# A two-layer graph transformer: 250 instead of 500 nodes in the dense share of the graph convolutions

## The chip, the cores and the metric

The kernel runs on one core of a Trainium2 chip. The metric is the device time of one execution in microseconds (us). Engines go by their short names: PE is TensorE (matmuls; PEld is its weight load), DVE is VectorE, ACT is ScalarE, POOL is GpSimd, SP is SyncE, which only issues DMAs. DRAM is the chip's memory; SBUF and PSUM are the core's own memories.

## The reference

The input is `x`, 2500 nodes by 256 features, and 40000 edges (`src`, `dst`), sorted by `dst`. All is float32. Two layers follow each other; each adds to `x` a graph operator and an attention-like mixer, both taken of the layer-normed `x`, and then a mixture of experts.

```python
edge_index = jnp.stack([src, dst])
xn = _layernorm(x, axis=-1)
x = x + _L0_gnn_ref(xn, ...) + _L0_mix_ref(xn[None], ...)[0]
x = x + _L0_ffn_ref(_layernorm(x, axis=-1)[None], ...)[0]      # 8 experts, each token to 2
xn = _layernorm(x, axis=-1)
x = x + _L1_gnn_ref(xn, ...) + _L1_mix_ref(xn[None], ...)[0]
x = x + _L1_ffn_ref(_layernorm(x, axis=-1)[None], ...)[0]      # 8 experts, each token to 1
```

The change lies in `_L1_gnn_ref`, two graph convolutions in a row, which the kernel computes beside `_L1_mix_ref`, a transformer of four layers (linear attention, then a feed-forward net 256 to 1024 to 256):

```python
deg = in-degree + 1 (a self loop);  dis = rsqrt(deg);  norm = dis[src] * dis[dst]
h = segment_sum((x @ W1)[src] * norm, dst) + b1          # self loops among the edges
h = where(h >= 0, h, alpha * h)
h = segment_sum((h @ W2)[src] * norm, dst) + b2
```

## The kernel before, in words

The 2500 nodes are held as 20 tiles of P = 125 nodes, in 5 groups of GT = 4 tiles (GC = 500 nodes). X is the running sum in SBUF.

**Layer 0.** The edges are turned into adjacency matrices by one-hot products, one group of 500 destinations at a time, and multiplied with the split features (`neighbours`, L458). While group 0 is in work, `between` (L1074) also writes its adjacency matrix, with the identity added on its diagonal blocks for the self loops, to DRAM as float32: `adj0`, 20 blocks of 125 sources by 500 destinations (L708, L1088 to L1094). The other groups' matrices are not kept.

**Ranks.** For the nodes outside group 0, `rank_nodes` (L326) sorts by in-degree: a histogram over 64 bins, matmuls for the prefix sums, and one indirect DMA per tile that writes each node's record to its rank in DRAM (`byrank`, L374). The ranks are cut into rows of 128. `MOST` (L34) gives the longest neighbour list that each row is prepared for; `rank_edges` (L381) fetches as many edges for each rank, one indirect DMA per row (L401), and leaves the neighbours' numbers in `nbr` and the nodes' own in `node`. If some node had more edges than its row allows, the count would not add up (L415 to L427) and a slow path would run. These steps are generators, which the loops of layer 0 and of its experts advance (L1095, L1227).

**The convolutions.** Everything after L1254 belongs to them and to the transformer. `conv_in` (L1287) writes x @ W1 times `dis` to the DRAM table `tabs[0]`. Each convolution then sums rows of its table in two ways:

- `dense` (L1272) for the 500 nodes of group 0: for each of the 20 source tiles it loads the adjacency block (`e`) and the table rows (`t`) and makes four products of 125 by 125 with 125 by 256 (L1281) into two PSUM tiles. It is cut into ten steps, and each transformer layer takes five of them (L1560, L1650).
- `gathers` (L1299) for the other 2000: for each row of 128 ranks, one indirect DMA for the node itself and one per neighbour place, 128 table rows of 1 KB each (L1313), on POOL's queue. They come in steps of SUM = 4; DVE adds each step to the first (L1325), then folds the four into one (L1329, L1331). POOL runs up to LEAD = 4 steps ahead, in LEAD + 1 buffers. `finish` then writes the row's sums: in the first convolution through `rectified` (L1340, bias and leaky rectifier) to `tabs[1]`, in the second to `sums2`, each with one indirect DMA (L1335).

The second convolution starts when the first one's last rows are written. After the fourth layer `conv_out` (L1387) takes the sums group by group: group 0 straight from PSUM (L1393), the others from `sums2` by a DMA on POOL's queue (L1395); it scales, transposes, multiplies by W2 and adds to X. The last mixture of experts follows.

**The order of the work** beside the transformer is dealt out by a clock that exists only while the program is traced. Each gather step has a due time: GATHER = 1.27 times the gathers so far (plus one per row), plus LANDING = 12, counted from the convolution's start; the second starts SEAM = 30 after the first's last step. The transformer calls `conv_step(now)` (L1369) at many places, and there all steps are emitted that are due:

```python
conv_step(LAYER * l - 0.6 * AHEAD * (NG - 1 - g) / NG)                                 # L1503, keys
conv_step(LAYER * l + AHEAD * i / NT * 0.7)                                            # L1552, context
conv_step(LAYER * l + AHEAD + (LAYER - 1.6 * AHEAD) * (g + step / (nj + GT)) / NG)     # L1604, feed-forward
```

So LAYER = 237 says how many units of that clock a transformer layer lasts. What a step puts on DVE stands in DVE's queue, in order, between the transformer's own instructions. Whatever is left at the end is emitted at L1671, ahead of `conv_out`.

Of the kernel before, what the change touches and what calls it, by code (L numbers as in the profile page):

```python
# [10 lines left out]
F32 = mybir.dt.float32  # L11
# [3 lines left out]
ALU = mybir.AluOpType  # L15
AX = mybir.AxisListType
# [3 lines left out]
D = 256  # L20
# [13 lines left out]
MOST = (42, 24, 22, 21, 19, 18, 18, 17, 16, 15, 15, 14, 13, 12, 11, 10)  # L34
# [7 lines left out]
LAYER = 237.0  # L42
# [24 lines left out]
def gps_kernel(ctx: ExitStack, tc: tile.TileContext, a, out):  # L67
# [258 lines left out]
    def rank_nodes(pool):  # L326

        nt = NT - GT
# [3 lines left out]
        V.tensor_scalar(upto, cnt[:, GT:NT], float(NBIN - 1), None, ALU.min)  # L332
# [6 lines left out]
        for g in range(NG - 1):  # L339
            ps = psum2.tile([128, 2, GT, NBIN], F32, tag="cx", name="ps")  # L340
            flat = oh[:, g * GT:(g + 1) * GT, :].rearrange("p i b -> p (i b)")
            T.matmul(ps[:P, 0].rearrange("p i b -> p (i b)"), below, flat, start=True, stop=True)
            T.matmul(ps[:, 1].rearrange("p i b -> p (i b)"), ones, flat, start=True, stop=True)
            for k in range(GT):
                V.tensor_tensor(rank[:, g * GT + k, :], ps[:P, 0, k, :], full[:P], ALU.add)
                V.tensor_tensor(full, ps[:, 1, k, :], full, ALU.add)
            yield
# [16 lines left out]
        G.tensor_copy(rec[:, :, 0:1], token[:, GT:, None])  # L364
        G.tensor_copy(rec[:, :, 1:2], cnt[:, NT + GT:2 * NT, None])
        G.tensor_copy(rec[:, :, 2:3], dis[:, GT:, None])
# [14 lines left out]
    def rank_edges(pool):  # L381
# [36 lines left out]
        V.tensor_reduce(hits[:P, 1:2], cnt[:, 0:GT], AX.X, ALU.add)  # L418
# [289 lines left out]
    adj0 = dram.tile([P, NT, GC], F32, name="adj0")  # L708
# [358 lines left out]
    for g in range(NG):  # L1067
# [6 lines left out]
        def between(k):  # L1074
# [179 lines left out]
    with tc.tile_pool(name="hid", bufs=8) as hid, tc.tile_pool(name="conv", bufs=1) as conv:  # L1254
# [17 lines left out]
        def dense(tab, sums):  # L1272

            for i in range(0, NT, 2):
                t = hid.tile([128, 2 * D], F32, tag="h", name="t")[:P].rearrange("p (k d) -> p k d", k=2)
                move(nc.sync, t, by_node(tab)[:, i:i + 2, :])
                for k in range(2):
                    e = hid.tile([128, 2 * D], F32, tag="h", name="e")[:P, :GC]
                    move(nc.sync, e, adj0[:, i + k, :])
                    for d in range(GT):  # L1280
                        T.matmul(sums[d // 2][:, d % 2, :], e[:, d * P:(d + 1) * P], t[:, k, :],  # L1281
                                 start=(i + k == 0 and d % 2 == 0), stop=(i + k == NT - 1 and d % 2 == 1))
# [71 lines left out]
        def first_group(sums):  # L1354

            by2 = conv.tile([P, GT], F32, name="by2")
            V.tensor_tensor(by2, dis[:, 0:GT], dis[:, 0:GT], ALU.mult)
            for d in range(GT):
# [706 lines left out]
```

## Time and profile before

| | us |
|---|---|
| median of three runs | 1825.29 (1821.66 to 1827.47) |
| the profiled execution | 1823.58 |
| its span (first to last instruction) | 1821.6 |
| mean granted PE clock | 0.978 |

Stretches of the profiled execution, from the span's start, with what PE and POOL were busy in each:

| stretch, us | what runs | PE | POOL |
|---|---|---|---|
| 0 to 300 | layer 0: scan, graph operator, mixer, gates, ranks | 261.7 | 108.6 |
| 300 to 490 | first mixture of experts | 169.5 | 88.1 |
| 490 to 594 | keys, context, attention of transformer layer 0 | 94.9 | 41.5 |
| 594 to 764 | feed-forward of layer 0 | 169.0 | 131.9 |
| 764 to 843, 843 to 1015 | layer 1: attention, feed-forward | 75.8, 169.7 | 60.7, 111.3 |
| 1015 to 1095, 1095 to 1265 | layer 2 | 76.2, 169.3 | 49.0, 127.4 |
| 1265 to 1350, 1350 to 1520 | layer 3 | 78.2, 169.6 | 65.8, 77.0 |
| 1520 to 1550 | `conv_out` | 24.6 | 0.2 |
| 1550 to 1822 | second mixture of experts | 260.0 | 81.3 |

PE is the busiest engine, 94% of the span. "Busy" counts an instruction's own time; the pauses between POOL's gathers, which issue the next DMA, count as idle. A releaser is what ended an engine's idle time, as inferred from the semaphores.

### The profile page before, as it was taken

The page shows a single profiled execution, that of the slowest core. Times are in us where ns is not written, and L with a number is a line of the kernel's source. Part 1 is how long each engine was busy: PE and PEld are TensorE (multiplying, and loading weights), DVE is VectorE, ACT ScalarE, POOL GpSimd, SP SyncE. Part 2 cuts the span into 40 slices and gives each one's busy share as a digit, 9 for nine tenths or more (in the row PEclk, how much of TensorE's full clock was granted, in tenths as well). Part 3 has the DMA queues.
Part 4 walks back from the last instruction along what each step waited for, and adds up shares of the span by engine and source line. Part 5 has one row for each costly group of instructions (what it writes and reads, how often), then busy time and mean ns, then how long its engine had stood idle before and what let it go on. Part 6 is the DMA issues. An engine that isn't in the chain of part 4 may idle for free. (4 is left out here: it accounts for less than half of the span.)

```text
span 1821.6 us, 24708 instructions
## 1 busy us (share of the span) xinstructions
PE 1718.5 (94%) x8081; PEld 1256.1 (69%) x8081; DVE 1005.7 (55%) x2906; ACT 655.3 (36%) x1170; POOL 942.7 (52%) x942
## 2 busy tenths in 40 slices
PE   4889999898799999999999999999999998999998
PEld 3646667787687667786776886676867767446767
DVE  8777744333554467576566374574646536333323
ACT  5743312222551434433335324343424331443220
POOL 2004483365217777777772666777777510144222
PEclk8999999999899999999999999999999999999999
DMA  5121156778436534554331664567543210621100
GB/s 141 57 60 44 37 169 197 241 222 233 131 107 170 97 93 112 165 146 143 98 102 49 195 120 138 158 176 202 156 139 92 73 50 33 216 65 48 32 21 29
DMA packets 131697, 216.59 MB, mean 119 GB/s; under 512 B 32876, under 2 KB 97570, under 8 KB 131303
## 3 DMA queue, kind: packets, MB, share of 16 engines
q0 software_dynamic: 51264, 111.78, 23.6%
q1 hardware_dynamic: 77990, 99.17, 18.4%
q10 hardware_dynamic: 2304, 3.94, 1.0%
q8 instruction: 70, 1.15, 0.3%
q14 instruction: 69, 0.56, 0.1%
HBM read 169.44 MB, written 47.79 MB: 119 GB/s over the span
## 5 line engine op out<-in xcount | busy, mean ns | idle before, releaser
L1313 POOL DMA_INDIRECT piece<-tab,nbr x574 | 591.8, 1031 | 204.4 <-issue 155.2
L1609 PE MATMUL mm<-xT,w 128*128 128x500 f32 x640 | 290.2, 596 | 2.8 <-ACT xT L487 2.8
L1620 PE MATMUL mm<-w,h 128*125 128x256 f32 x1280 | 288.0, 379 | 0.1
L1620 PEld LDWEIGHTS mm<-w,h 128*125 128x125 f32 x1280 | 238.0, 188 | 43.2 <-issue 8.8
L1609 PEld LDWEIGHTS mm<-xT,w 128*128 128x128 f32 x640 | 121.8, 195 | 119.4 <-issue 106.7
L1612 ACT ACTIVATE h<-mm,bf 128x500 f32<-128x500 f32 x160 | 106.8, 675 | 199.6 <-PE mm L1609 199.5
L1325 DVE TENSOR_TENSOR piece<-piece 128x1024 f32<-128x1024 f32 (+3 forms) x130 | 146.2, 1127 | 11.9 <-DMA piece<-tab,nbr 11.5
L465 PE MATMUL pa<-edges,xb 125*128 125x500 bf16 x600 | 138.7, 383 | 5.5 <-DVEq L959 3.6
L1622 DVE TENSOR_TENSOR tok<-tok,mm 125x256 f32<-125x256 f32 x80 | 33.5, 418 | 136.5 <-PE mm L1620 136.3
L1029 POOL DMA_INDIRECT back<-yo,xs x60 | 60.2, 1004 | 92.1 <-DVE yo L1027 52.7
L1577 DVE TENSOR_TENSOR tok<-tok,po 125x256 f32<-125x256 f32 x80 | 30.1, 418 | 138.2 <-PE po L1574 137.8
L465 PEld LDWEIGHTS <-xb 125*128 125x128 bf16 x600 | 58.6, 101 | 68.4 <-issue 11.5
L1012 PE MATMUL mm<-xc,wt 128*128 128x128 f32 x688 | 88.2, 283 | 15.5 <-DMA wt<-in_expert_in_dram 13.0
L1012 PEld LDWEIGHTS mm<-xc,wt 128*128 128x128 f32 x688 | 83.7, 198 | 17.4 <-issue 7.7
L1016 ACT ACTIVATE h<-mm,wt 128x128 f32<-128x128 f32 x172 | 49.1, 368 | 118.0 <-issue 65.4
L809 ACT CAST edges<-mm 125x500 bf16<-125x500 f32 x100 | 65.1, 790 | 70.6 <-PE mm L806 70.5
L494 ACT ACTIVATE tok<-tok,less,rstd 125x256 f32<-125x256 f32 x140 | 72.6, 591 | 38.4 <-DVE less L492 33.7
L1022 PE MATMUL py<-w,h 128*128 x344 | 82.8, 385 | 1.8 <-ACT h L1016 1.8
L487 ACT ACTIVATE xT<-mm,mixc 128x500 f32<-128x500 f32 x80 | 57.2, 765 | 68.1 <-PE mm L482 66.5
L1971 PE MATMUL py<-wd,taken 128*128 x368 | 80.9, 380 | 0.5 <-DVE taken L1961 0.5
L1499 PE MATMUL mm<-wa,xT 128*125 128x256 f32 x320 | 77.8, 398 | 1.9 <-ACT xT L487 1.2
L1971 PEld LDWEIGHTS py<-wd,taken 128*128 128x128 f32 x368 | 69.7, 190 | 11.3 <-issue 1.4
(484 smaller groups left out, 3010.9 us busy)
## 6 DMA issues: line engine op xcount, KB each, us to landing
wt<-in_expert_in_dram SPq DMA_DIRECT2D x43, 514.0 KB
sorted<-nothing SPq DMA_DIRECT2D x5, 2031.2 KB
piece<-tab,nbr POOLq DMA_INDIRECT x574, 3.1
e<-adj SPq DMA_DIRECT2D x40, 218.8 KB
w<-in_L_mix_W_dram SPq DMA_DIRECT2D x8, 1024.0 KB
wd<-in_L_ffn_Wd_dram SPq DMA_DIRECT2D x8, 1024.0 KB
t<-tab SPq DMA_DIRECT2D x20, 224.0 KB
adj<-wide SPq DMA_DIRECT2D x20, 218.8 KB
```

The costliest lines, as they stand in the source:

```text
L465: T.matmul(pa[c], table[:, k, n, c * 128:(c + 1) * 128], edges[:, k, :], start=(k == 0 and n == 0), stop=(k == NT - 1 and n == 2))
L494: S.activation(rows[:, k, :D], src[:, lo + k, :D], AF.Identity, bias=less[:, k:k + 1], scale=rstd[:, k:k + 1])
L809: S.copy(o.rearrange("p s (n d) -> p n s d", d=BD), ps[:P].rearrange("p (n s d) -> p n s d", n=BD, d=BD))
L1012: T.matmul(ps[:, j * TS:(j + 1) * TS], wt[:, c * F0 + j * 128:c * F0 + (j + 1) * 128], xc[:, c * TS:(c + 1) * TS], start=(c == 0), stop=(c ...
L1022: T.matmul(ps, h[:, j * TS:(j + 1) * TS], w2[:, ds(e, 1), j, :], start=(j == 0), stop=(j == NJ - 1))
L1313: G.indirect_dma_start(out=t[:, i, :], out_offset=None, in_=tab, in_offset=bass.IndirectOffsetOnAxis(ap=by, axis=0))
L1325: V.tensor_tensor(total[:, :m, :], total[:, :m, :], t[:, :m, :], ALU.add)
L1499: T.matmul(ps[:, k * D:(k + 1) * D], hT[:, c, (i + k) * P:(i + k + 1) * P], wk[:, c, :], start=(c == 0), stop=(c == 1))
L1609: T.matmul(ps, w1[:, c, j * 128:(j + 1) * 128], fT[:, c, g * GC:(g + 1) * GC], start=(c == 0), stop=(c == 1))
L1612: S.activation(h, ps, AF.Gelu, bias=bf[:, l, j:j + 1])
L1620: last["product"] = T.matmul(ps, hh[j][:, k * P:(k + 1) * P], w2[:, j, :], start=(j == 0), stop=(j == nj - 1)).ins
L1971: T.matmul(ps, h[:, j * TS:(j + 1) * TS], wd[:, ds(e, 1), j, :], start=(j == 0), stop=(j == nj - 1))
```

## The change

The dense share covers the first ND = 2 tiles (250 nodes) in place of the first group of four (500). The nodes from 250 on are ranked and gathered: 2250 in 18 rows of 128 in place of 2000 in 16 (2000 / 128 = 15.6, 2250 / 128 = 17.6), and `MOST` gets two more entries: it sums to 320 in place of 287. The adjacency in DRAM is half as wide, as are its copies and loads; `dense` makes two products per source tile in place of four; `first_group` rectifies two tiles in place of four. `rank_nodes` has a half-full fifth round, in one step of the generator with what follows. `conv_out` now also fetches the second half of group 0 from `sums2` by a DMA on POOL's queue. LAYER goes from 237 to 253, so the clock that deals out the steps runs faster against the transformer.

```diff
-MOST = (42, 24, 22, 21, 19, 18, 18, 17, 16, 15, 15, 14, 13, 12, 11, 10)
+MOST = (42, 24, 22, 21, 20, 19, 18, 17, 17, 16, 15, 15, 14, 14, 13, 12, 11, 10)
+ND = 2
+DC = ND * P
...
-LAYER = 237.0
+LAYER = 253.0
...
-        nt = NT - GT
+        nt = NT - ND
...
-        for g in range(NG - 1):
+        for lo in range(0, nt, GT):
+            n = min(GT, nt - lo)
...
-            yield
+            if n == GT:
+                yield
...
-    adj0 = dram.tile([P, NT, GC], F32, name="adj0")
+    adj0 = dram.tile([P, NT, DC], F32, name="adj0")
...
-                w = odd.tile([P, GC], F32, tag="wide", name="wide", bufs=3)
-                S.copy(w, edges[:, k, :])
-                if k < GT:
+                w = odd.tile([P, DC], F32, tag="wide", name="wide", bufs=3)
+                S.copy(w, edges[:, k, :DC])
+                if k < ND:
...
-                    e = hid.tile([128, 2 * D], F32, tag="h", name="e")[:P, :GC]
+                    e = hid.tile([128, 2 * D], F32, tag="h", name="e")[:P, :DC]
                     move(nc.sync, e, adj0[:, i + k, :])
-                    for d in range(GT):
+                    for d in range(ND):
                         T.matmul(sums[d // 2][:, d % 2, :], e[:, d * P:(d + 1) * P], t[:, k, :],
...
-            for d in range(GT):
+            for d in range(ND):
                 o = conv.tile([128, D], F32, tag="sums", name="sums", bufs=3)[:P]
...
+            lo = ND if g == 0 else 0
+            move(nc.gpsimd, s[:, lo:, :], by_node(sums2)[:, g * GT + lo:(g + 1) * GT, :])
+            V.tensor_tensor(s[:, lo:, :], s[:, lo:, :], by[:, lo:, :].to_broadcast([P, GT - lo, D]), ALU.mult)
             if g == 0:
-                for c in range(2):
-                    V.tensor_tensor(s[:, 2 * c:2 * c + 2, :], twice[0][c], by[:, 2 * c:2 * c + 2, :].to_broadcast([P, 2, D]), ALU.mult)
-            else:
-                move(nc.gpsimd, s, by_node(sums2)[:, g * GT:(g + 1) * GT, :])
-                V.tensor_tensor(s, s, by.to_broadcast([P, GT, D]), ALU.mult)
+                for c in range(0, ND, 2):
+                    n = min(2, ND - c)
+                    V.tensor_tensor(s[:, c:c + n, :], twice[0][c // 2][:, :n, :], by[:, c:c + n, :].to_broadcast([P, n, D]), ALU.mult)
```

More of the change, by code (lines that the diff above doesn't have):

```diff
@@ L331, in rank_nodes @@
         upto = pool.tile([P, nt], F32, name="upto")
-        V.tensor_scalar(upto, cnt[:, GT:NT], float(NBIN - 1), None, ALU.min)
+        V.tensor_scalar(upto, cnt[:, ND:NT], float(NBIN - 1), None, ALU.min)
         oh = pool.tile([P, nt, NBIN], F32, name="oh")
@@ L338, in rank_nodes @@
         yield
-        for g in range(NG - 1):
+        for lo in range(0, nt, GT):
+            n = min(GT, nt - lo)
             ps = psum2.tile([128, 2, GT, NBIN], F32, tag="cx", name="ps")
[L341 to L345, printed above, removed]
+            flat = oh[:, lo:lo + n, :].rearrange("p i b -> p (i b)")
+            T.matmul(ps[:P, 0, :n].rearrange("p i b -> p (i b)"), below, flat, start=True, stop=True)
+            T.matmul(ps[:, 1, :n].rearrange("p i b -> p (i b)"), ones, flat, start=True, stop=True)
+            for k in range(n):
+                V.tensor_tensor(rank[:, lo + k, :], ps[:P, 0, k, :], full[:P], ALU.add)
                 V.tensor_tensor(full, ps[:, 1, k, :], full, ALU.add)
-            yield
+            if n == GT:
+                yield
         upper = full[:P]
@@ L363, in rank_nodes @@
         G.memset(rec, 0.0)
-        G.tensor_copy(rec[:, :, 0:1], token[:, GT:, None])
-        G.tensor_copy(rec[:, :, 1:2], cnt[:, NT + GT:2 * NT, None])
-        G.tensor_copy(rec[:, :, 2:3], dis[:, GT:, None])
+        G.tensor_copy(rec[:, :, 0:1], token[:, ND:, None])
+        G.tensor_copy(rec[:, :, 1:2], cnt[:, NT + ND:2 * NT, None])
+        G.tensor_copy(rec[:, :, 2:3], dis[:, ND:, None])
         none = pool.tile([128, 4], F32, name="none")
@@ L417, in rank_edges @@
         V.tensor_reduce(hits[:, 0:1], hit, AX.X, ALU.add)
-        V.tensor_reduce(hits[:P, 1:2], cnt[:, 0:GT], AX.X, ALU.add)
+        V.tensor_reduce(hits[:P, 1:2], cnt[:, 0:ND], AX.X, ALU.add)
         V.tensor_tensor(hits[:, 0:1], hits[:, 0:1], hits[:, 1:2], ALU.add)
@@ L1277, in dense @@
                 for k in range(2):
-                    e = hid.tile([128, 2 * D], F32, tag="h", name="e")[:P, :GC]
+                    e = hid.tile([128, 2 * D], F32, tag="h", name="e")[:P, :DC]
                     move(nc.sync, e, adj0[:, i + k, :])
-                    for d in range(GT):
+                    for d in range(ND):
                         T.matmul(sums[d // 2][:, d % 2, :], e[:, d * P:(d + 1) * P], t[:, k, :],
-                                 start=(i + k == 0 and d % 2 == 0), stop=(i + k == NT - 1 and d % 2 == 1))
+                                 start=(i + k == 0 and d % 2 == 0), stop=(i + k == NT - 1 and (d % 2 == 1 or d == ND - 1)))
                 if i + 2 == NT and tab is tabs[0]:
@@ L1354, in first_group @@
         def first_group(sums):
-            by2 = conv.tile([P, GT], F32, name="by2")
-            V.tensor_tensor(by2, dis[:, 0:GT], dis[:, 0:GT], ALU.mult)
-            for d in range(GT):
+            by2 = conv.tile([P, ND], F32, name="by2")
+            V.tensor_tensor(by2, dis[:, 0:ND], dis[:, 0:ND], ALU.mult)
+            for d in range(ND):
                 o = conv.tile([128, D], F32, tag="sums", name="sums", bufs=3)[:P]
```

## The prediction

> **What bounds the kernel now.** I read the page's busy shares first, then the stretches of the four transformer layers, where the convolutions run, then POOL's groups inside each convolution, and last POOL's and DVE's waits. Page, busy shares and the two dense rows:
>
> ```profile
> PE 1718.5 (94%) x8081; PEld 1256.1 (69%) x8081; DVE 1005.7 (55%) x2906; ACT 655.3 (36%) x1170; POOL 942.7 (52%) x942
> ```
>
> The stretches; each line is attention or feed-forward of one layer (busy time of PE, PEld, DVE, ACT, POOL):
>
> ```profile
> 594.00:764.00 170.00, 168.97 (x660) 118.25 (x658) 102.61 (x297) 67.22 (x106) 131.89 (x126) 0.99 0.45 107
> 764.00:843.00 79.00, 75.81 (x375) 63.34 (x376) 59.27 (x134) 30.95 (x50) 60.70 (x61) 1.00 0.61 173
> 1015.00:1095.00 80.00, 76.18 (x379) 63.75 (x377) 50.00 (x110) 28.49 (x45) 49.00 (x49) 0.98 0.70 155
> 1265.00:1350.00 85.00, 78.22 (x379) 65.25 (x378) 54.43 (x118) 28.90 (x45) 65.79 (x64) 0.97 0.62 173
> ```
>
> PE is full in the feed-forward (169.0 of 170) and loses 3 to 7 us per attention stretch. So PE sets the length. But 52% is a poor picture of POOL. Its groups in the first convolution (540 to 967) and in the second (997 to 1449):
>
> ```profile
> L1313 POOL DMA_INDIRECT piece<-tab,nbr x287 | 297.1, 1035 | 87.5 <-issue 76.8 <-DMA piece<-tab,nbr 1.5 <-DVE neg L1347 0.9
> L1335 POOL DMA_INDIRECT tab<-sums,node x14 | 16.8, 1201 | 4.7 <-issue 3.4 <-DVE sums L1348 0.7 <-DVE fk L1424 0.3
> ...
> L1313 POOL DMA_INDIRECT piece<-tab,nbr x287 | 294.6, 1027 | 116.9 <-issue 78.3 <-DVE piece L1325 18.1 <-DVE qs L1545 10.3
> L1335 POOL DMA_INDIRECT sums<-sums,node x14 | 14.3, 1023 | 4.3 <-issue 3.0 <-DVE tok L1577 0.6 <-DVE tok L1622 0.3
> ```
>
> Almost all of its idle time is "issue", 0.30 us before every gather: back to back, a gather costs 0.95 + 0.30 us and more. In the first convolution POOL never waits longer than that: it is full from 540 to 966, as full as PE. The order of time at the turn between the convolutions shows where it has air:
>
> ```profile
> 964.99 0.95 POOL L1313 DMA_INDIRECT piece<-tab,nbr  x1 [0.30 <-issue]
> 966.64 1.01 POOL L1335 DMA_INDIRECT tab<-sums,node  x1 [0.71 <-DVE sums L1348]
> 973.84 1.01 POOL L1335 DMA_INDIRECT tab<-sums,node  x1 [6.18 <-DVE y L176]
> 993.69 0.98 POOL L1335 DMA_INDIRECT tab<-sums,node  x1 [18.84 <-DVE y L178]
> 998.25 0.99 POOL L1313 DMA_INDIRECT piece<-tab,node  x1 [3.57 <-DMA tab<-sums,node]
> ```
>
> 28 us lie there, since the last steps stand late in DVE's queue. At the end the last scatter goes out at 1476 and the feed-forward ends at 1520: 44 us of air. DVE's side:
>
> ```profile
> DVE piece L1325 <- DMA piece<-tab,nbr: 11.5, 5, 6.1
> ```
>
> DVE waits for a gather 11.5 us in all, in five places. So two engines run in step, and the change moves work from PE to POOL.
>
> **The change, part by part.**
>
> *Removed from PE.* L1281 has 76.0 us in 320 records (two per float32 product), 19.3 us in each attention stretch; half is 38.0 us, 9.5 per layer. Some of these products fill holes there, so the gain lies between 9.5 and 5 (the 3.2 to 6.8 us of holes a stretch grow by what filled them); I take 8, hence 32 us. If nothing else waited, the feed-forward of layer 3, ended at 1519.6, would end at 1487.6.
>
> *Added to POOL: the gathers.* 320 - 287 + 2 = 35 more per convolution, and two more scatters. First convolution before: 540.35 to 965.94 is 425.6 us; 13 scatters of 1.20 + 0.30 are 19.5, which leaves 406.1 / 303 = 1.340 per gather. After: 338 x 1.340 + 15 x 1.50 = 475.4, so its gathers end at 1015.8, 50 us later. Second before: 998.25 to 1447.44 is 449.2; 13 scatters of 1.32 are 17.2 and waits for buffers and landings 18.1 + 10.3 + 3.5 = 31.9, which leaves 1.320 per gather; after, 338 x 1.320 + 15 x 1.32 = 466.0. Bounds of the price: 1.256 (bare, no DVE instruction in the way) and 1.37 (eight more adds of L1325, 73 for 65, that each stop POOL for their whole 1.21 us: 9.7 / 338 = 0.03 more). I take 1.34 and 1.32, since the same DVE lines run beside them.
>
> The long gathers are those that start under a DVE add with both inputs in SBUF: 0.95 us bare, 1.96 us at 603.16 under L1325 (603.07 to 604.29). In the first convolution the excess is 297.1 + 16.6 - 303 x 0.953 = 25 us over 65 adds, 0.38 each; 8 more adds are 3 us, and the price per gather above has them. The Trainium skill, "SBUF — State Buffer", section Who interferes with whom, says that DVE with two SBUF inputs and a reading GpSimd exclude each other for the whole instruction; this speaks against the change. By that rule alone 8 adds of 1.21 us would cost up to 10 us a convolution in place of 3.
>
> *The turn.* Last add to first gather of the second convolution took 998.25 - 989.9 = 8.4 us; with a landing 2.1 us after the gather's end, the second starts at 1015.8 + 2.1 + 8.4 = 1026.3, against 998.25. The 28 us of air are gone.
>
> *The steps dealt out.* The last step of the second convolution is due at 958 of the clock's 988 units (before 864 of 924). In a feed-forward 189 units now pass in some 170 us, so a gather is due every 1.27 x 170 / 189 = 1.14 us and POOL delivers one in 1.34: over the 149 gathers due there POOL falls behind by 30 us, of which its lead of about 25 us (a piece landed at 966 was added at 990) takes the first part. Then DVE waits in its queue for the landing, and behind the waiting add stand attention's sums (L1577), the statistics (L187), and behind those ACT's rows (L494) and PE's transposes (L482), which wait now already: PE is held. The attention stretches (64 units in some 70 us) give little back. At the second's start its first adds are due late and POOL waits for buffers: before 6.4 and 7.1 us, now some 10. So its gathers end at 1026.3 + 466.0 + 10 = 1502.3.
>
> *The end, two ways.* Over the table: from last add (1473.4) to the rows for `conv_out` landed (1484.4) 11.0 us passed; after, 1502.3 + 2.1 + 11.0 = 1515.4. Over PE: the last point where a late DVE holds PE is the statistics of group 4, at 928 units; 30 units are 23 gathers, 31 us, so POOL's side is met at 1502.3 - 31 + 2.1 = 1473.4; one add (1.2) and the chain as before (L1577 at 1472.7 to L482 at 1481.0, 8.3) give 1482.9, and the rest of the layer (1481.0 to 1519.6, 38.6) gives 1521.5. The later one counts: +1.9 us against 1519.6.
>
> *DVE.* 16 more adds of 1.13 us and four more pairs of folds (0.69 and 0.42) in 980 us, of which it works 570: hidden, except that an add in the chain above delays it by 1.2. Landings come up to 7 us late (longest wait 6.1), and in step with POOL each counts once. Between 0 and 8 us; I take 3.
>
> *Ranks.* Two more record scatters (1.19 + 0.30 each) in POOL's fullest early stretch (71.5 of 100 us), two more edge gathers (1.0 + 0.3 each) between the experts' scatters, two small DVE pairs of 0.45 us, a half matmul round: between 0 (PE does other work there) and 6; I take 1.5. The two further generator steps fit into the loop's 23 calls (21 needed).
>
> *The rest.* Adjacency copies half as wide (ACT, 13.2 us of CASTs halved, beside a PE that waits 1.9 us for ACT there), half the block loads on SP's queue (5 MB less), two fewer `rectified`, one more table load for group 0 on POOL's queue (0.7 us twice), whose landing is in the 1515.4: -1 to +1, taken as 0. If that cover is gone, because the loads land after the feed-forward, `conv_out` waits for them.
>
> *Sum.* 1.9 + 3 + 1.5 = +6.4 on the profiled execution's 1823.6 (span 1821.6 and 2.0 around it): 1830. That execution lies 1.7 us under the median of the runs, 1825.3, so I forecast 1832.
>
> **The rivals.**
>
> *POOL keeps up, PE's gain comes through* (the other side). If gathers came at the bare 1.256, the first would end at 540.35 + 338 x 1.256 + 22.5 = 987.4, the second at 987.4 + 10.5 + 444.3 + 10 = 1452, and PE would set the end at 1488 to 1500: 1795 to 1805. It decides at a mean price of about 1.31, where POOL's two chains are 17 us shorter. For it: a waiting DVE does less beside the gathers. Against: the adds that lengthen gathers all stay.
>
> *Waits pass to PE whole.* If every late add holds PE until the last one, the 30 units behind the last step (27 us of feed-forward) follow the landing at 1504.4 plus add: 1533, +13, with the small terms +18: 1843; with a price of 1.35, 1852. For it: the transposes have no reserve (L482 waits for ACT's rows 19.9 us in all). Against: in group 4 PE and ACT run 14 us without DVE.
>
> *The late adds stay hidden.* DVE is idle 40% and catches up between chains; then the table alone counts, 1515.4: -4, with 1.5 for the ranks 1823.
>
> *It isn't what it says.* A row of ranks with more edges than MOST would run the slow path. The reference's edges, sorted by in-degree in 18 rows from node 250 on, start rows with 32, 22, 21, 20, 19, 18, 18, 17, 16, 16, 15, 15, 14, 13, 13, 12, 11, 9: none is over. No chance given.
>
> **How the numbers follow.** Forecast 0.50 (its own range 1824 to 1840), POOL keeps up 0.21, waits pass whole 0.18, late adds hidden 0.11. A measurement tells some 0.3%, 5.5 us, from no change: 1819.8 to 1830.8. Faster: 0.21 and a sliver, 0.22. Same: 0.11 and 0.15 of the forecast's 0.50, about 0.26. Slower: 0.52. The range leaves out the upper tail of the last case and the far half of the fast one: 1810 to 1852.
>
> **What would show it.** Right: 676 gathers at 1.31 to 1.35 us with no wait for L1325's buffers in the feed-forward; the second convolution's first gather at 1020 to 1032, its last at 1495 to 1510; DVE's waits for pieces up from 11.5 to over 60 us; PE under 165 of 170 us busy in the feed-forwards, L1281 at 38 us. Wrong: a gather price near 1.26; adds moved late in DVE's queue so that PE stays full and POOL ends alone after the feed-forward; first scatters of layer 0's experts visibly later.

## The result, and the profile after

The changed kernel takes 1877.57 us (median of 4 runs, 1875.72 to 1878.49) against 1824.76: slower by 2.74%, ratio 1.0274 with a 95% interval of 1.0255 to 1.0292. The forecast, 1832 in 1810 to 1852, had the sign and an eighth of the size. The profiled execution took 1878.3 us, its span 1876.3, at a mean granted clock of 0.955 (before 0.978).

The page's busy shares:

```profile
PE 1706.5 (91%) x7925; PEld 1238.4 (66%) x7925; DVE 1026.8 (55%) x2934; ACT 651.6 (35%) x1170; POOL 1034.5 (55%) x1022
```

PE is 12 us less busy, not 38, and 67 us more idle. Where, the stretches say (start and end; length; busy time and instructions of PE, PEld, DVE, ACT, POOL; granted clock; DMA share; GB/s): first the four feed-forwards, then the attention of layers 1 to 3.

```profile
595.00:787.00 192.00, 176.93 (x663) 122.09 (x663) 106.71 (x307) 68.67 (x109) 149.03 (x142) 0.94 0.44 106
871.00:1057.00 186.00, 173.13 (x658) 119.74 (x658) 109.84 (x319) 69.78 (x111) 133.55 (x129) 0.95 0.36 101
1135.00:1324.00 189.00, 175.88 (x662) 122.07 (x662) 102.53 (x293) 65.64 (x103) 137.64 (x132) 0.94 0.55 159
1402.00:1572.00 170.00, 169.84 (x656) 118.35 (x656) 87.84 (x199) 57.64 (x86) 122.68 (x117) 0.99 0.35 99
787.00:871.00 84.00, 69.59 (x331) 57.44 (x331) 56.45 (x126) 29.58 (x48) 65.10 (x63) 0.91 0.52 150
1057.00:1135.00 78.00, 67.31 (x337) 56.02 (x335) 45.57 (x105) 28.07 (x44) 45.14 (x48) 0.96 0.64 130
1324.00:1402.00 78.00, 67.34 (x333) 55.76 (x334) 51.68 (x114) 28.43 (x45) 59.55 (x61) 0.96 0.55 158
```

The loss has one address: the first three feed-forwards are 191.3, 185.7 and 188.4 us long, before 170.7, 172.6 and 170.4. That is 52 us of the 54.7 by which the two profiled spans differ. About 36 us of it are more idle time, the rest matmuls that run at a clock of 0.94 and not 0.99. The fourth feed-forward is full, as before. The second surprise stands in the last three lines. PE's work in the attention stretches fell by 6, 9 and 10 us, since half of the dense products are gone, and yet these stretches take 84.9, 78.2 and 78.1 us, before 78.8, 79.6 and 84.2: 1 us gained in all.

Why, the end of such a stretch shows. Layer 2, PE before (two lines), then PE and DVE after (start, duration, what; in brackets the idle time before it and what ended it):

```profile
1082.50 7.07 PE L1281 MATMUL da<-t,e 125*125 125x256 f32 x32
1092.08 2.16 PE L482 MATMUL mm<-ident,tok 125*128 125x125 f32 x8 [2.51 <-ACT tok L494]
...
1121.29 3.19 PE L1539 MATMUL mm<-wq,xT 128*125 128x256 f32 x14
1132.49 2.16 PE L486 MATMUL mm<-ident,tok 125*128 125x125 f32 x8 [8.02 <-ACT tok L498]
...
1119.76 0.75 DVE L1582 TENSOR_TENSOR tok<-tok,po 125x256 f32<-125x256 f32 x2 [1.93 <-PE po L1579]
1123.57 1.19 DVE L1329 TENSOR_TENSOR piece<-piece 128x1024 f32<-128x1024 f32 x1
1129.30 1.22 DVE L1329 TENSOR_TENSOR piece<-piece 128x1024 f32<-128x1024 f32 x1
1131.58 0.16 DVE L496 SCALAR_TENSOR_TENSOR less<-mv,rstd 125x4 f32<-125x4 f32 x1
```

From attention's sums (L1582) to `less` (L496) DVE works for 12.0 us without a pause, mostly at the statistics and softmaxes of the transformer itself, and waits for no gather. PE needs the rows that follow for its transposes (L486). Before, dense products filled that time; now PE stands there. In front of the feed-forwards of layers 1 to 3 these holes are 8.0, 8.0 and 8.2 us, before 1.5, 2.5 and 2.5.

The waits of the whole execution (engine, line, what it waited for: us in all, times, longest), before 33.7, 11.5, 19.9, 20.2 and 18.1 us in this order:

```profile
ACT tok L498 <- DVE less L496: 73.0, 25, 14.6
DVE piece L1329 <- DMA piece<-tab,nbr: 64.3, 13, 11.7
PEld mm L486 <- ACT tok L498: 49.0, 29, 8.6
ACT b L1348 <- DVE sums L1349: 44.5, 10, 16.0
POOL piece L1317 <- DVE piece L1329: 35.3, 8, 15.5
```

DVE waits for gathers, ACT's rows for DVE, PE for ACT's rows (the holes just shown are in these sums too); and POOL, which should be the engine that is late, waits 35 us for DVE. How a wait for a gather reaches PE is seen in order of time, in layer 1's feed-forward, POOL, DVE, ACT and PE:

```profile
1027.39 1.84 POOL L1317 DMA_INDIRECT piece<-tab,nbr  x1 [0.30 <-issue]
1038.29 1.00 POOL L1339 DMA_INDIRECT tab<-sums,node  x1 [7.75 <-DVE mv L190]
...
1027.18 2.36 DVE L1329 TENSOR_TENSOR piece<-piece 128x1024 f32<-128x1024 f32 x2 [9.69 <-DMA piece<-tab,nbr]
1033.46 0.96 DVE L1329 TENSOR_TENSOR piece<-piece 128x768 f32<-128x768 f32 x1 [3.92 <-DMA piece<-tab,nbr]
1037.27 0.42 DVE L189 BATCH_NORM_STATS2 st<-tok 125x6 f32<-125x256 f32 x1
1041.16 0.16 DVE L496 SCALAR_TENSOR_TENSOR less<-mv,rstd 125x4 f32<-125x4 f32 x1
...
1041.36 1.09 ACT L498 ACTIVATE tok<-tok,less,rstd 125x256 f32<-125x256 f32 x2 [14.63 <-DVE less L496]
1042.36 0.66 ACT L1617 ACTIVATE h<-mm,bf 128x500 f32<-128x500 f32 x1
...
1043.06 1.22 PE L1625 MATMUL mm<-w,h 128*125 128x256 f32 x2 [11.16 <-ACT h L1617]
```

POOL issues the first convolution's last gathers without a pause. DVE has come to their additions 9.7 us too soon and stands. Behind them, in its queue, stands the next group's statistics (L189), so `less` is late, so ACT stands 14.6 us in front of the rows (L498); and behind the rows, in ACT's queue, stands the gelu (L1617) of the group in work, for which PE's second product waits 11.2 us. Then POOL waits 7.8 us for DVE to finish the sums that it has to scatter.

POOL's groups in the first convolution (548 to 1030) and in the second (1044 to 1552):

```profile
L1317 POOL DMA_INDIRECT piece<-tab,nbr x320 | 336.3, 1051 | 100.3 <-issue 82.9 <-DMA piece<-tab,nbr 3.7 <-DVE piece L1329 3.4
...
L1317 POOL DMA_INDIRECT piece<-tab,nbr x320 | 328.1, 1025 | 131.8 <-issue 84.1 <-DVE piece L1329 31.6 <-DMA piece<-tab,nbr 4.7
```

The first takes 480.9 us for 338 gathers, scatters included 1.423 us each, nearly all of it POOL's own (before 425.6 for 303, 1.405). So that price hardly moved. The second takes 507.0 us, since POOL stands 31.6 us for buffers that DVE's late additions hold.

### The profile page after: what moved, and what is told of

Same layout as the page of the kernel before. It is cut to its first block, busy times and chain, and to the rows that moved or that the text cites. A ratio compares the mean times of both kernels' runs of the same rounds, so it can differ in the third digit from the quotient of the medians.

```text
span 1876.3 us, 24566 instructions
## 1 busy us (share of the span) xinstructions
PE 1706.5 (91%) x7925; PEld 1238.4 (66%) x7925; DVE 1026.8 (55%) x2934; ACT 651.6 (35%) x1170; POOL 1034.5 (55%) x1022
## 5 line engine op out<-in xcount | busy, mean ns | idle before, releaser
L1317 POOL DMA_INDIRECT piece<-tab,nbr x640 | 664.4, 1038 | 232.1 <-issue 167.0
L1625 PE MATMUL mm<-w,h 128*125 128x256 f32 x1280 | 299.4, 388 | 28.9 <-ACT h L1617 28.8
L1625 PEld LDWEIGHTS mm<-w,h 128*125 128x125 f32 x1280 | 243.9, 193 | 76.8 <-ACT h L1617 33.2
L1329 DVE TENSOR_TENSOR piece<-piece 128x1024 f32<-128x1024 f32 (+3 forms) x146 | 163.0, 1120 | 64.6 <-DMA piece<-tab,nbr 64.3
L1617 ACT ACTIVATE h<-mm,bf 128x500 f32<-128x500 f32 x160 | 106.6, 675 | 197.1 <-PE mm L1614 196.9
L1016 PE MATMUL mm<-xc,wt 128*128 128x128 f32 x688 | 89.4, 285 | 15.1 <-DMA wt<-in_expert_in_dram 10.9
L1582 DVE TENSOR_TENSOR tok<-tok,po 125x256 f32<-125x256 f32 x80 | 30.2, 417 | 127.9 <-PE po L1579 127.5
L498 ACT ACTIVATE tok<-tok,less,rstd 125x256 f32<-125x256 f32 x140 | 72.8, 591 | 73.1 <-DVE less L496 73.0
L486 PE MATMUL mm<-ident,tok 125*128 125x125 f32 x360 | 58.0, 301 | 44.0 <-ACT tok L498 41.0
L1016 PEld LDWEIGHTS mm<-xc,wt 128*128 128x128 f32 x688 | 84.7, 200 | 17.6 <-issue 8.3
L486 PEld LDWEIGHTS mm<-ident,tok 125*128 125x128 f32 x360 | 45.4, 155 | 57.9 <-ACT tok L498 49.0
L550 POOL DMA_INDIRECT sorted<-rows,to x40 | 50.0, 1250 | 58.0 <-DVE to L545 45.3
```

Source lines behind the costliest of these rows:

```text
L486: T.transpose(ps[:, k * P:(k + 1) * P], src_of(k)[:, c * 128:(c + 1) * 128], ident[:P, :P])
L498: S.activation(rows[:, k, :D], src[:, lo + k, :D], AF.Identity, bias=less[:, k:k + 1], scale=rstd[:, k:k + 1])
L1016: T.matmul(ps[:, j * TS:(j + 1) * TS], wt[:, c * F0 + j * 128:c * F0 + (j + 1) * 128], xc[:, c * TS:(c + 1) * TS], start=(c == 0), stop=(c ...
L1317: G.indirect_dma_start(out=t[:, i, :], out_offset=None, in_=tab, in_offset=bass.IndirectOffsetOnAxis(ap=by, axis=0))
L1329: V.tensor_tensor(total[:, :m, :], total[:, :m, :], t[:, :m, :], ALU.add)
L1617: S.activation(h, ps, AF.Gelu, bias=bf[:, l, j:j + 1])
```

## What was tried

Theory at the start: POOL is full, the additions come due in DVE's queue before their gathers have landed, and the wait passes along DVE and ACT to PE. Rivals: the halved dense products alone (a cover gone), the changed LAYER alone, ACT's bias rows (L1348) in its queue, the later ranks, the ring of pieces. All ratios are against the kernel before on the same chip; the changed kernel's is 1.0274.

**Half of the dense products, alone.**

```diff
-                    for d in range(GT):
+                    for d in range(GT if i + k == 0 else 2):
...
-                                 start=(i + k == 0 and d % 2 == 0), stop=(i + k == NT - 1 and d % 2 == 1))
+                                 start=(i + k == 0 and d % 2 == 0),
+                                 stop=((i + k == 0 and d == 3) if d > 1 else (i + k == NT - 1 and d == 1)))
```

> The kernel before, with the dense products of destination tiles 2 and 3 left out for 19 of the 20 source tiles (so the sums of nodes 250 to 499 are incomplete); gathers, ranks, loads and LAYER as before. It is PE's gain by itself. Theory A (the dense products are ordinary PE work; my prediction's step): 8 us per layer, so about 1793, 32 less than before. Theory B (most of them fill holes in which PE would wait for the statistics and ACT's rows, which the trace of after shows: holes of 5.5 to 8 us ahead of the first feed-forward transposes of every layer, 1.5 to 2.5 before): 2.5 us per layer, so 1810 to 1817.

1836.85 us, ratio 1.0063 (1.0041 to 1.0084): slower, and no theory had it. Layer 0's feed-forward began at 583.1 and not 593.2; of these 10 us, 5.8 lay ahead of the first gather (534.6 for 540.4) and so ahead of every dense product, which leaves 4. Layer 1's attention lost 19 (98.0 for 78.8 us), layers 2 and 3 changed by 1.4 us at most: there PE's holes in front of L482 are 8.4 and 9.4 us, as in the changed kernel, and no wait for a gather stands in them either. The loss, in order of time, DVE, ACT and POOL:

```profile
816.22 0.41 DVE L1349 SCALAR_TENSOR_TENSOR sums<-sums,neg 125x256 f32<-125x256 f32 x1
832.12 0.48 DVE L1346 SCALAR_TENSOR_TENSOR sums<-da,by,b 125x256 f32<-125x256 f32 x1 [15.49 <-DMA tab<-sums,node]
...
832.64 0.51 ACT L1345 ACTIVATE b<-b1row,disr 128x256 f32<-128x256 f32 x1 [17.21 <-DVE sums L1346]
833.05 1.04 ACT L1568 COPY qt<-mm 128x500 f32<-128x500 f32 x2
...
829.57 1.01 POOL L1336 DMA_INDIRECT tab<-sums,node  x1 [0.30 <-issue]
```

The dense nodes' sums use the same ring of three buffers (`sums`) as the ranks' sums. Here they came when a rank's scatter stood behind 13 gathers in POOL's queue; DVE stood 15.5 us until it had landed, ACT's copy for PE's next product behind it.

**All four products again, in the changed kernel.**

```diff
-DC = ND * P
+DC = GC
...
-                    for d in range(ND):
+                    for d in range(GT):
                         T.matmul(sums[d // 2][:, d % 2, :], e[:, d * P:(d + 1) * P], t[:, k, :],
-                                 start=(i + k == 0 and d % 2 == 0), stop=(i + k == NT - 1 and (d % 2 == 1 or d == ND - 1)))
+                                 start=(i + k == 0 and d % 2 == 0), stop=(i + k == NT - 1 and d % 2 == 1))
```

> The changed kernel, with the adjacency written and loaded 500 wide and all four products per source tile made as before, the extra two unused. 18 rows of ranks and LAYER 253 stay. It is the gathers' and ranks' cost without PE's gain. Theory A (PE's gain is there, 8 us per layer, and the gathers cost the rest): 1877 + 32 = 1909. Theory B (the removed products were cover) and theory C (late gathers set the pace, PE has time to spare): 1872 to 1887, and the holes ahead of the first transposes shrink from 5.5 to 8 us to under 4.

1875.15 us, ratio 1.0281 (1.0259 to 1.0304): the same as without them. Attention of layers 2 and 3:

```profile
1052.00:1131.00 79.00, 76.27 (x380) 63.88 (x379) 45.67 (x105) 28.78 (x45) 46.29 (x48) 1.00 0.70 141
1318.00:1396.00 78.00, 75.62 (x378) 63.34 (x376) 51.49 (x114) 27.88 (x44) 59.71 (x61) 1.00 0.62 175
```

PE has 9 and 8 us more work in them and they are as long: the holes in front of L486 are 1.1 and 1.2 us. In the changed kernel the products cost nothing, and taking them away gains nothing.

**LAYER alone, from both sides.**

```diff
-LAYER = 237.0
+LAYER = 253.0
```

> The kernel before, with LAYER 253 in place of 237 alone: the same gathers, dealt out faster. Theory C (a step due before its gather has landed stops DVE, and behind it ACT and PE): POOL, full already in the first convolution, can't follow; DVE's waits for pieces rise from 11.5 us to 30 or more and the time to 1832 to 1850. Theory D (dealing is harmless, the number of gathers alone costs): 1822 to 1828, waits under 15.

1856.06 us, ratio 1.0177 (1.0155 to 1.0199): the kernel before with nothing but the constant changed loses 31 us. Its feed-forwards are 187.4, 170.0, 184.3 and 167.7 us long, and DVE waits 51.9 us for pieces (11.5). The other way round, the changed kernel with 237:

> The changed kernel with LAYER 237 as before: the steps are dealt out more slowly, the last is due at 958 units where the layers end at 924, so about 27 gathers are left for after the last feed-forward. Theory C (the dealing is what costs): DVE's waits for pieces inside the layers fall from 64 us to under 30, the feed-forward of layer 3 ends 20 to 35 us sooner than in after (1572), and some 35 us of gathers lie bare ahead of the last products: 1865 to 1880. Theory E (POOL's chain sets the end whatever the dealing): the last gather at 1551 plus or minus 5 and the time at 1872 to 1882.

1883.66 us, ratio 1.0315 (1.0283 to 1.0346). The feed-forwards are nearly full (171.3, 172.0, 181.5, 171.2), but layer 1's attention has 95.8 us, with the ring's wait of e1 again (8.4 us), and the stretch behind the last feed-forward 336.8 for 299.0: the additions that are dealt out more slowly are left over at the end, where nothing covers them.

**Four smaller suspects.** More buffers for the bias rows:

```diff
-            b = conv.tile([128, D], F32, tag="b", name="b", bufs=2)[:n]
+            b = conv.tile([128, D], F32, tag="b", name="b", bufs=4)[:n]
```

> The changed kernel with four buffers in place of two for the scaled bias b in rectified. In after, ACT stands 44.5 us (longest 16.0) at that instruction, waiting for DVE to free a buffer, with gelus behind it, and PE has holes of 8.6 and 11.2 us at 769 and 1043 that end with a gelu. Theory F (ACT is stopped by the bias ring): both holes go, 15 to 25 us with the clock that follows them, so 1852 to 1862. Theory C alone (ACT would stand at the next row of the norms anyway): 1872 to 1880.

1872.94 us, 1.0282 (1.0253 to 1.0311): no change; ACT's wait for the sums stays (43.2 us for 44.5). An earlier start of the second convolution's additions:

```diff
-SEAM = 30.0
+SEAM = 5.0
```

> The changed kernel with SEAM 5 in place of 30: the second convolution's steps are due 25 units sooner. In after POOL waits 35 us for buffers, most of it at the start of the second convolution (15.5 at 1084 to 1099). Theory E (POOL's chain sets the end): those waits go, the last gather comes 15 to 25 us sooner, the time falls to 1855 to 1867. Theory C (steps due too early stop DVE): DVE's waits in the second convolution grow instead of POOL's, the time stays within 6 of 1877 or rises.

1890.66 us, 1.0374 (1.0336 to 1.0411): 1% slower than the changed kernel's 1.0274. POOL's waits for DVE's additions fell from 35.3 to 20.4 us and the second convolution from 507.0 to 481.7, so that its gathers ended at 1526.6 for 1551.1, and still layer 2 got longer (its attention 89.1 us for 78.2), since DVE's waits for pieces rose to 74.5. So the end of POOL's chain does not set the time by itself. What counts is how late each piece is against its place in DVE's queue. One generator step less among the ranks:

```diff
-            if n == GT:
+            if lo < 3 * GT:
                 yield
```

> The changed kernel with the fourth and fifth round of the rank counts in one generator step, so that the record scatters can go out one call sooner. In before four of them went out at 201, in a hole of POOL; in after all 18 stand at 230 to 255 in front of the last token scatters, and the first mixture of experts starts 8.5 us later. Theory G (the record scatters delay the token scatters): the first expert product comes 5 to 9 us sooner and the time is 1867 to 1873. Rival (the delay has another cause): 1875 to 1880.

1873.39 us, 1.0277 (1.0249 to 1.0305). The first experts' products came at 294.6 for 296.8 (before the change 288.3); but without this edit they came at 293.7 in e5 and 298.5 in e6, so an effect isn't shown, neither there nor at the end. And the bias rows on DVE in place of ACT:

```diff
-            S.activation(b, b1row[:n], AF.Identity, scale=by)
+            V.tensor_scalar(b, b1row[:n], by, None, ALU.mult)
```

> The changed kernel with the 20 scaled bias rows of the rectified sums made on DVE (one more operation of about 0.3 us each) and not on ACT, so that nothing of the convolutions stands in ACT's queue. Theory P with holds passed on in two ways (ACT's own wait for the sums, 44.5 us in all, and ACT's rows waiting for DVE's statistics, 73.0 us): the first way goes; of the four long holes of PE in the feed-forwards the one at 769 us (8.6 us) goes, the others stay: 1862 to 1874. Rival B (ACT in order behind the bias is the cause): the products' waits on ACT's h fall from 33 us to under 8, feed-forwards 170 to 178, the time 1835 to 1850.

1876.6 us, 1.0291 (1.0258 to 1.0325): no change, and even the hole at 769 us stays. The waits:

```profile
ACT tok L498 <- DVE less L496: 90.5, 23, 14.9
PE mm L1625 <- ACT h L1617: 29.7, 6, 11.0
```

ACT's wait for the sums (44.5 us) is gone; its wait in front of the rows has grown from 73.0 to 90.5, PE's products wait for the gelus as before (28.8), and the time is the same. Freeing one instruction gains nothing while those behind it wait for DVE as well.

**Dealt by POOL's true price.**

```diff
-GATHER = 1.27
+GATHER = 1.34
```

> The changed kernel with GATHER 1.34 in place of 1.27, what a gather takes in the trace: the steps are dealt out at POOL's own pace, the last due at about 1005 units of 988, so a few are left for the end. Theory C (late steps stop DVE, ACT and PE): DVE's waits for pieces fall from 64 us to under 30 and the layers get 15 to 30 us shorter, of which some 15 are given back ahead of the last products: 1858 to 1872. Theory E (POOL's chain sets the end): 1874 to 1882.

1872.63 us, 1.0277 (1.025 to 1.0304): again the same time, in another shape. Layer 1's feed-forward and the stretch after the last one:

```profile
855.00:1027.00 172.00, 171.20 (x663) 118.48 (x662) 108.32 (x317) 68.49 (x110) 128.36 (x122) 0.99 0.36 104
1532.00:1600.00 68.00, 35.01 (x145) 25.11 (x144) 42.00 (x157) 4.97 (x9) 22.85 (x27) 0.75 0.40 113
```

The fourth feed-forward ends at 1532 and not 1572, and what was won lies bare behind it: PE works 35 of 68 us there. With the seam earlier as well:

```diff
-GATHER = 1.27
+GATHER = 1.34
...
-SEAM = 30.0
+SEAM = 10.0
```

> The changed kernel with GATHER 1.34 in place of 1.27 and SEAM 10 in place of 30. Theory P (POOL's pace sets the layers: a gather takes POOL 1.34 us, the dealing counts 1.27, so DVE's adds come due before their gathers have landed; dealt slower, the adds are late at the end instead): with GATHER 1.34 alone the feed-forwards of layers 1 and 2 were 172 and 182 us, but the stretch behind the last feed-forward was 330 us in place of 299, since the second convolution's adds came late and POOL waited 26 us for them. An earlier seam lets POOL go on there: the last stretch 305 to 315 us, the feed-forwards 172 to 190, the time 1848 to 1862. Rival L (the look-ahead of 16 gathers is too short, whatever the pace): the seam only moves the holds, 1872 within 5.

1855.7 us, 1.0175 (1.0144 to 1.0205), as forecast: the stretch at the end is 313.0 us, the feed-forwards 183.9, 171.5, 181.8 and 171.3. And with about as many gathers as before the change (each rank's last two neighbours are left out):

```diff
-GATHER = 1.27
+GATHER = 1.34
...
-            steps = [(j, k) for j in range(NR) for k in range(0, MOST[j] + 1, SUM)]
+            steps = [(j, k) for j in range(NR) for k in range(0, MOST[j] - 1, SUM)]
...
-                m = min(SUM, MOST[j] + 1 - k)
+                m = min(SUM, MOST[j] - 1 - k)
...
-                yield GATHER * (sum(min(SUM, MOST[i] + 1 - b) for i, b in steps[:n + 1]) + j)
+                yield GATHER * (sum(min(SUM, MOST[i] - 1 - b) for i, b in steps[:n + 1]) + j)
...
-                if k + SUM > MOST[j]:
+                if k + SUM > MOST[j] - 2:
```

> The changed kernel with GATHER 1.34 and each rank's last two neighbours never gathered (36 of 338 gathers less in each convolution, so 302, about as many as before the change; the output is not the reference's). Theory P: POOL has 50 us less in each convolution, so that it keeps the pace and ends in time: feed-forwards 170 to 176 us, the stretch behind the last one 297 to 303, the time 1815 to 1832. Rival D (the halved dense products alone make the holes, as they did with the other ranks left at 237): 1835 to 1850, with 15 to 25 us of PE idle in front of layer 1's feed-forward.

1854.43 us, 1.0154 (1.0123 to 1.0185), slower than either theory's number. One half of theory P holds: the end is covered again (301.3 us for e8's 330.5). The other half misses: layer 1's attention is 97.8 us long, 15.1 us of it DVE's wait for the ring of sums as in e1, and two feed-forwards still have 177 and 178 us.

**Smaller pieces, further ahead.**

```diff
-SUM = 4
-LEAD = 4
+SUM = 2
+LEAD = 12
...
-                    V.tensor_tensor(total[:, 0:2, :], total[:, 0:2, :], total[:, 2:4, :], ALU.add)
```

> The changed kernel with pieces of 2 rows (SUM 2) and 12 of them fetched ahead (LEAD 12): POOL may run 24 gathers in front of DVE's adds in place of 16, with the same dealing by GATHER 1.27. Theory P: the waits of POOL on DVE (35 us) go, but the adds still come due faster than POOL gathers, so DVE's waits for pieces stay at 45 to 70 us and the time at 1862 to 1880. Rival L (look-ahead too short): both waits fall under 20 us, feed-forwards 170 to 178, the time 1825 to 1845.

1838.18 us, 1.0068 (1.0039 to 1.0096): 39 us of the 53 are back, the rival's range of time, though not all of its signs (the first feed-forward is too long for it, and the waits of DVE for pieces and of POOL for DVE, 23.2 and 21.8 us, lie just above its 20). The feed-forwards are 181.3, 175.3, 176.5 and 171.1 us. POOL's gathers and DVE's additions in the first convolution:

```profile
L1317 POOL DMA_INDIRECT piece<-tab,nbr x320 | 320.6, 1002 | 97.5 <-issue 69.8 <-DMA piece<-tab,nbr 4.6 <-DVE piece L1329 3.4
...
L1329 DVE TENSOR_TENSOR piece<-piece 128x512 f32<-128x512 f32 x146 | 99.0, 685 | 23.3 <-DMA piece<-tab,nbr 22.7
```

DVE works more (99.0 us of full additions, before 59 of 1.21 us, 71.5), but a gather is cheaper: 1.002 for 1.051 us, and the convolution 460.8 for 480.9. POOL waits for DVE's additions 3.4 us there in both kernels, so this part of the gain belongs to the cheaper gathers, by argument at least, and not to the look-ahead. To part the two, the smaller pieces were run with only 16 gathers ahead (e13, and again e17):

```diff
-SUM = 4
-LEAD = 4
+SUM = 2
+LEAD = 8
...
-                    V.tensor_tensor(total[:, 0:2, :], total[:, 0:2, :], total[:, 2:4, :], ALU.add)
```

> The changed kernel with pieces of 2 rows (SUM 2) but still 16 gathers ahead (LEAD 8). Theory L (the look-ahead of 16 gathers is too short for POOL's falling behind and DVE's stops, and 24 are what took 39 us off): no gain from the finer pieces alone, POOL's waits for DVE stay near 35 us, DVE's for pieces over 45, the time 1864 to 1880. Rival F (finer pieces are what helped: an addition waits for 2 landings and not for 4): 1834 to 1850, POOL's waits for DVE under 25 us.

> The changed kernel with pieces of 2 rows and 16 gathers ahead, as in e13_pieces_2_ahead_16, whose neighbour, the kernel before, took 2117 us there in place of 1825 (its engines stood for instructions, and not for each other), so that neither theory could be read from it. Theory L (the look-ahead counts): 1864 to 1880, ratio 1.022 to 1.030, POOL's waits for DVE near 35 us. Rival F (the finer pieces count): 1834 to 1850, ratio 1.005 to 1.014, POOL's waits for DVE under 25 us.

With them went e1's kernel with a larger ring of sums (e14), the kernel before with e11's edit (e15, and again e18), and the changed kernel with e11's edit, that ring and GATHER 1.30 (e16). The ring, in both places:

```diff
-                    sums = conv.tile([128, D], F32, tag="sums", name="sums", bufs=3)
+                    sums = conv.tile([128, D], F32, tag="sums", name="sums", bufs=5)
```

> The kernel before with half of the dense products left out as before (its output is not the reference's: the dense nodes of two tiles get only the first source tile's share) and 5 buffers in place of 3 for the ranks' sums, which the dense nodes' rows share. Theory S (the 12 us lost with half the products were a collision in this ring: the dense nodes' rows came earlier, and DVE stood 15.5 us until POOL's scatter of a rank had read its buffer): the stretch in front of layer 1's feed-forward falls from 98 to 78 to 82 us, the time 1814 to 1824, so half of the products is worth at most 10 us, of a layer or two. Rival C (the chains of DVE and ACT that the products covered make the hole, not the ring): 98 us stay, the time 1832 to 1842.

> The kernel before with pieces of 2 rows and 24 gathers ahead. Theory L: before, POOL kept up, DVE waited 11.5 us for pieces and POOL some 18 us for DVE in the middle of its work, and the feed-forwards were full (170.1 to 172.6 us), so nothing is to be had: 1816 to 1828. Rival F: the additions are more operations on DVE (300 more), whose cost would show here: 1828 to 1840.

> The kernel before with pieces of 2 rows and 24 gathers ahead, as in e15_before_ahead_24, which was 1.3% faster than the kernel before among runs of 2117 us. Theory L: where the feed-forwards are full (170 to 173 us) there is nothing to be had but a few us of DVE's 11.5 of waiting: ratio 0.996 to 1.001, 1816 to 1828 us. Rival: the gain of 1.3% is the look-ahead's in any state: ratio 0.983 to 0.991.

> The changed kernel with pieces of 2 rows, 24 gathers ahead, 5 buffers for the sums and GATHER 1.30. Theory L with P (what is left in the feed-forwards at 24 ahead, 181.3, 175.3 and 176.5 us, is the pace being still too quick by 1.34 to 1.27): feed-forwards 171 to 177 us, the last stretch 298 to 306, the time 1822 to 1836. Rival (the slower dealing shows at the end at once): the last stretch 308 to 318, the time 1838 to 1850.

In both batches of these six the kernel before itself took 2117 and 2088 us, with engines standing for "issue" where they had not before, so their times cannot be put beside the others. Measured: e13 2147.99 us, ratio 1.0168 (1.0096 to 1.0241); e17, the same kernel, 2119.68, 1.0199 (1.0127 to 1.027); e14 2095.75, 0.9914 (0.9877 to 0.9952); e15 2091.28, 0.9872 (0.9794 to 0.995); e18, the same kernel, 2061.82, 0.9893 (0.9845 to 0.9941); e16 2157.41, 1.0188 (1.0114 to 1.0262). What can be read: with five buffers DVE's wait for the ring of sums is gone from the list (17.7 us in e1), while layer 1's attention is long there for other reasons; and with that ring the halved products are 0.9% faster than the kernel before, where e1 was 0.6% slower. Smaller pieces and a longer look-ahead made the kernel before 1.1 to 1.3% faster in those conditions; whether they do at 1825 us is open, and with it whether a version beats both kernels. Open too is how much of e11's gain is the look-ahead. The cheaper gather at least doesn't seem to need it: with 16 ahead (e13) a gather of the first convolution took 1.002 us too, though in those conditions.

## One rule behind the runs

What a layer lasts in time follows from the dealing. A layer holds LAYER units; in the first convolution each gather is dealt out at GATHER times (gathers + rows) / gathers units, 1.27 x 356 / 338 = 1.338 in the changed kernel. If POOL needs 1.423 us for it, the additions and the gathers stay in step only if a layer lasts 253 x 1.423 / 1.338 = 269 us. The mean from one feed-forward's start to the next, over three layers, was 268.9. In the table the last column runs from the last feed-forward's end to PE's last product.

| kernel | LAYER | POOL, us per gather, first convolution | units per gather | layer by the rule | layer measured | behind the last feed-forward |
|---|---|---|---|---|---|---|
| before | 237 | 1.405 | 1.337 | 249.0 | 252.1 | 296.6 |
| before, LAYER 253 (e3) | 253 | 1.421 | 1.337 | 269.0 | 262.5 | 298.5 |
| after | 253 | 1.423 | 1.338 | 269.1 | 268.9 | 299.0 |
| after, four products (e2) | 253 | 1.424 | 1.338 | 269.4 | 266.4 | 301.5 |
| after, LAYER 237 (e4) | 237 | 1.449 | 1.338 | 256.8 | 258.9 | 336.8 |
| after, SEAM 5 (e6) | 253 | 1.421 | 1.338 | 268.8 | 272.9 | 298.6 |
| after, GATHER 1.34 (e8) | 253 | 1.437 | 1.411 | 257.7 | 257.2 | 330.5 |
| after, 1.34, SEAM 10 (e9) | 253 | 1.427 | 1.411 | 255.8 | 256.1 | 313.0 |
| after, smaller pieces (e11) | 253 | 1.363 | 1.338 | 257.8 | 255.7 | 298.2 |

The price per gather is read from the same run and holds POOL's waits for DVE (12.6 of e4's 490 us are one such wait), so part of the agreement is built in. What carries the rule is that LAYER and GATHER were changed and the price hardly moved, and the layer followed them (before and e3; after, e4 and e8). It holds for the mean: in e3 the three layers are 274.6, 248.7 and 264.2 us. It explains two things. The change asks for 16 units more a layer from a POOL that is no quicker, so the mean layer grows to 269. And dealing more slowly shortens the layers but leaves additions for the end: what the table's sixth column gains, the last one loses (e4, e8). The 70 gathers more are 100 us of POOL at 1.423 us each; the air that the prediction found, 28 us at the turn and 44 at the end, is 72. What the rule does not explain is that the halved products gain nothing in layers 1 to 3; that is the cover which they were for DVE's own work (e1, e2).

## Why the prediction was wrong, step by step

- *What bounds the kernel.* PE full in the feed-forwards and POOL full from 540 to 966: right. That PE sets the length of the attention stretches too was wrong: their end is DVE's, whose statistics and softmaxes PE has to await.
- *Removed from PE, -32 us.* This step failed. PE's busy time in the three attention stretches did fall, by 25 us, and the stretches by 1. The bounds of 5 to 9.5 us a layer left out zero: the prediction knew that some of the products fill holes, but let them fill no more than 4.5 us a layer. Nearly all of them did: PE's wait for the rows (L486) grew from 1.5 to 2.5 us to 8 in each, as theory B of e1 had it. Only layer 0 gained: from the first gather to its feed-forward 46.9 us passed for 52.8 (48.5 in e1).
- *Added to POOL.* Nearly right. 676 gathers; by the prediction's own formula (480.9 - 15 x 1.50) / 338 = 1.356 us each in the first convolution for 1.340, and 1.328 in the second for 1.320. The excess over a bare gather of 0.953 rose from 25.0 to 31.5 us with 8 more additions: 0.8 us for each, between the prediction's 0.4 and its bound of 1.21. But the dealing alone moves it: in e3, without more additions, it is 28.0, and from there the 8 cost 0.4 each. The Trainium skill, "SBUF — State Buffer", section Who interferes with whom, has DVE with two SBUF inputs and a reading GpSimd exclude each other for the whole instruction. With additions of 0.685 us in place of 1.21 (e11) the excess was 16.1 us, which fits that rule, though the look-ahead changed with them; no run took the additions away.
- *The turn.* 10.5 us forecast, 14.9 measured: the last two scatters waited 7.8 and 2.2 us for DVE. The 28 us of air went, as said.
- *The steps dealt out.* This is the step that failed by most. It had the mechanism word for word, additions due faster than POOL delivers, DVE waiting, ACT's rows and PE held, and forecast over 60 us of DVE's waits (64.3). But it let a lead of 25 us and a single lateness of 30 us a feed-forward settle the matter, instead of asking what layer length keeps the two in step; and it let POOL run on at 466 + 10 us while PE was held. In fact PE, DVE and POOL stop each other: POOL's waits for buffers in the second convolution were 31.6 us, where the prediction had 10. Its last gather ended at 1551.1 and not 1502.3. The 48.8 us are: start 8.0 later (548.3), first convolution 5.5 longer, turn 4.4, second convolution 31.0.
- *The end, two ways.* From the last gather to the end of layer 3's feed-forward the prediction took 19.2 us (1502.3 to 1521.5); 21.1 were measured (1551.1 to 1572.2). That they agree is luck: layer 3's feed-forward was full (PE 169.8 of 170 us), so its end followed from its start at 1401.8 and not from the last gather; and in e6 the gathers ended 24 us earlier and the feed-forward 14 us later. The gelus (L1617) behind ACT's rows, through which the longest holds of PE went, were not in the chain.
- *DVE, +3.* The additions took 163.0 us for 146.2; what they cost by themselves was not measured.
- *Ranks, +1.5 of 0 to 6.* Out of bounds in the profile: the first experts' products came 8.5 us later (296.8 for 288.3; in e5 5.4, in e6 10.2). The delay is still there at the first gather (8.0 us), and then layer 0's attention, shorter by 5.9, makes most of it good: its feed-forward starts 2.0 us later.
- *The rest, 0.* Nearly so: the stretch behind the last feed-forward is 2.4 us longer.
- *The rivals.* "Waits pass to PE whole" was the nearest, with 1843 to 1852, and too low by the same chain. "POOL keeps up" is excluded: the price did not fall. "The late adds stay hidden" is too: DVE's late additions reach PE in three feed-forwards.
- *Its signs of being right.* The 676 gathers and DVE's waits came. The prices lie at the upper end of their range or just above it, and the second convolution's first and last gather, 1044.1 and 1551.1, came 12 and 41 us after the ends of theirs.

## What to carry to other kernels

Where one engine's work is dealt out beside another's by a fixed pace, work out the length that keeps them in step (units per piece of work against its measured price) before counting what either engine saves. Before taking work from the busiest engine, look at what ends the stretch in which it runs: where that is another engine's chain, the work was cover, and the engine stands in its place. A wait at the head of an in-order queue is not met once at the end, but at every stretch in which the pace is too quick; and dealing more slowly only moves it to where the work runs out of cover. Rows that share a small ring with a long queue of DMAs wait for that queue as soon as they come early.

## What was not expected of the hardware

A hole costs more than its length. The same matmuls of a feed-forward took PE 169.8 us at a granted clock of 0.99 (before, layer 0) and 176.9 at 0.94 with 15 us of holes among them; in layer 1 of e8, without holes, 171.2 at 0.99. In the changed kernel the hole of 8.6 us ends at 769.5; the granted clock is 0.50 from 768 to 774, 0.96 in the next 6 us and 1.00 after that. The Trainium skill, "TensorE: Matmul & The Clock Gate", section Part 1: The HAM clock gate, says that the clock is gated by how busy PE has lately been; these rows agree. In e11 halving the size of DVE's additions raised DVE's time for them (99.0 for 71.5 us in the first convolution) and lowered a gather's by 5%. And in two batches the same kernel before took 2117 and 2088 us: in the profile of e18 waits for "issue" or for something that the trace does not name add up to 313 us on DVE and 90 on PE, against 16 and 1 in the profile of before; why is not known.
